# Top-k search of an expert-choice router: bit masks counted by TensorE instead of accumulated comparisons, in one transformer-block kernel

## The chip, the cores and the metric

The kernel runs on one core of a Trainium2 chip. The metric is device time in microseconds, the median of several runs. A core has five engines with their own instruction queues: TensorE (PE in the profile; its weight loads are PEld), VectorE (DVE), ScalarE (ACT), GpSimd (POOL) and SyncE (SP, which here only issues DMAs). They meet through semaphores.

## The reference, cut to what matters

One transformer block over x of shape 8 x 1024 x 256: an attention (16 heads of 64) and then a mixture of experts in which each of 8 experts chooses its K = 512 best tokens out of all 8192:

```
logits = xf @ router_w + router_b           # 8192 x 8
scores = softmax(logits, axis=-1)
G, idx = top_k(scores.T, K)                 # for each expert its 512 best tokens
toks = xf[idx]
h1 = relu(toks @ w1[e] + b1[e])             # 512 x 1024
eo = h1 @ w2[e] + b2[e]                     # 512 x 256
y[idx] += eo * G                            # scattered back
```

Here xf is the normed and modulated attention output; the result is added to x under a gate. The order of the 512 tokens inside an expert does not matter, since their results are added to the rows they came from; ties at the threshold go to the lower token number.

## The kernel before, in words

The work has three parts, in this order.

1. *Attention*, 128 units of work with an order written out by hand. Its last batch also makes the routing scores of the last tokens: `out_route` multiplies with the router (L638), VectorE and ScalarE make the softmax (L643 to L664), and `out_store` has GpSimd copy the scores of 128 tokens into the tile `scores` (L671). Near its start, a small table `steps_of` is made: one row of four candidate offsets for each search step (L784 to L787).
2. *Search and ranks*, the part that is changed. Four transposes (L981) turn `scores` into the PSUM tile `p_sc`: 128 partitions, of which 16 belong to each expert, and 512 scores in each. VectorE copies it to `sc` (L985). The threshold of each expert, the 512th largest score, is then found in 15 steps of two bits, from the top of the fp32 bit pattern (scores are positive, so their order is that of their bits). A step compares all scores with three candidates (L996, each comparison also adds up its hits in a partition into `cnt`), one matmul with the 0/1 matrix `whole_h` adds `cnt` over the 16 partitions of an expert (L1001), `ge` counts how many candidates are reached by at least K scores (L1008), and `cand` is moved up by that many steps (L1013, in the last four steps L1019 and L1020, where float arithmetic would no longer be exact).
   The ranks: masks of scores above and equal to the threshold (L1030), running counts by two scans (L1037, L1043), counts of the partitions before by matmuls with `earlier` and `whole` (L1034, L1035, L1046), and from them the slot of each chosen token; four transposes (L1053) turn the slots back, and `lo` and `hi` are their low five and high bits (L1058, L1059).
3. *Experts*, again in an order written by hand. `entries` (L1075 to L1088) makes one-hot masks of `lo` and `hi`, `choose` (L1099) and `gather` (L1114 to L1123) turn them into token numbers and fetch the rows by indirect DMA; `turn` (L1136), `inner` (L1147) and `outer` (L1159) are the expert's matmuls; the results are added to the output by indirect DMA (L1168). Experts 1 to 7 have their entries made while the expert before them computes; for expert 0 all of it lies between the ranks and its first matmul.

The weights of the first four experts are loaded (L922, L924) while the search runs. In part 2 before the change, the order on each engine is a scheduler's; in the changed kernel, that of the code from the copy of `p_sc` on.

Of the kernel before, what the change touches and what calls it, by code (L numbers as in the profile page):

```python
# [28 lines left out]
F32 = mybir.dt.float32  # L29
BF16 = mybir.dt.bfloat16  # L30
F16 = mybir.dt.float16
I32 = mybir.dt.int32
AF = mybir.ActivationFunctionType
ALU = mybir.AluOpType
AX = mybir.AxisListType
# [3 lines left out]
P = 128  # L39
# [4 lines left out]
def adaln_block(  # L44
# [15 lines left out]
    nc = tc.nc  # L60
    B, S, D = x.shape
    H, _, _, N = w_qkv.shape
    E, _, F = w1.shape
    K = 512
# [6 lines left out]
    KT = K // P  # L71
# [4 lines left out]
    const = ctx.enter_context(tc.tile_pool(name="const", bufs=1))  # L76
    dram = ctx.enter_context(tc.tile_pool(name="dram", bufs=1, space=DRAM))

    ident = const.tile([P, P], F32, name="ident")
# [15 lines left out]

    scores = const.tile([P, KT, E, NTT // KT], F32, name="scores")
    modT = const.tile([P, 2 * KC, B], F32, name="modT")

    steps_of = const.tile([P, 16, 4], I32, name="steps_of")

    mod_d = dram.tile([B, 3 * D], F32, name="mod_d")
    gb_d = dram.tile([B, D], F32, name="gb_d")
# [65 lines left out]
    for i in range(NT // 2):  # L168
        t = work.tile([P, 2, D], F32, tag="p", name=f"x_first{i}", bufs=PB)
# [28 lines left out]
    def mod_silu():  # L198
        pt = ps_m.tile([P, KC, B], F32, tag="mm", name="pt")
        for k in range(KC):  # L200
            nc.tensor.transpose(pt[:, k, :], c_sb[:, k * P : (k + 1) * P], ident[:B, :B])
        nc.scalar.activation(sT, pt, AF.Exp, scale=-1.0)
        nc.vector.tensor_scalar_add(sT, sT, 1.0)
# [87 lines left out]
    def ln_out(b, t):  # L291
# [4 lines left out]
        if b == 0:  # L296
# [5 lines left out]
            for k in range(KC):  # L302
                nc.scalar.activation(  # L303
                    hTs[b][:, k, 2 * t * P : (2 * t + 2) * P], pt[:, k, :], AF.Identity,
                    bias=modT[:, k, b : b + 1], scale=modT[:, KC + k, b : b + 1],
# [463 lines left out]
    with tc.manual_schedule():  # L769
# [10 lines left out]
        ln_norm(0, NT // 2 - 1)  # L780
        for t in parts_of:
            nc.vector.memset(t, 0.0)

        nc.gpsimd.memset(steps_of, 0)  # L784
        nc.gpsimd.iota(steps_of[:, 14, :], pattern=[[1, 4]], base=0, channel_multiplier=0)
        for s in range(14):
            nc.vector.tensor_scalar(  # L787
                steps_of[:, s, :], steps_of[:, 14, :], 28 - 2 * s, None, op0=ALU.logical_shift_left
            )
        g = -1  # L790
        while g < 4 * NSU + LAG or steps:
            u, gm = divmod(g, 4)
# [105 lines left out]
        half = NT // 2  # L898
# [32 lines left out]
    C = NTT // KT  # L931
    lo = rt.tile([P, KT, E, C], I32, name="lo")
    hi = rt.tile([P, KT, E, C], I32, name="hi")
    LO = 32
# [12 lines left out]
    with tc.tile_pool(name="search", bufs=2) as se, tc.tile_pool(  # L947
        name="pos", bufs=1
    ) as po_, tc.tile_pool(name="se_ps", bufs=2, space=PSUM) as sps, tc.tile_pool(
        name="pos_ps", bufs=1, space=PSUM  # L950
    ) as pps:
        for dst, pattern, mult in (
            (iota_lo, [[1, LO]], 0), (iota_hi, [[1, HI]], 0), (part, [[0, 1]], 1),
            (first, [[P, KT], [P * KT, C]], 0),
        ):
            i = po_.tile(list(dst.shape), I32, name=f"i_{dst.name}")
            nc.gpsimd.iota(i, pattern=pattern, base=0, channel_multiplier=mult)
            nc.gpsimd.tensor_copy(dst, i)
        nc.vector.tensor_reduce(
            fold, ident.rearrange("p (g l) -> p l g", l=LO), AX.X, ALU.max  # L960
        )

        whole = po_.tile([P, E, C], F32, name="whole")
        nc.gpsimd.memset(whole, 1.0)
        for base, sign in ((0, 1), (C - 1, -1)):
            nc.gpsimd.affine_select(
                out=whole, in_=whole, pattern=[[-sign * C, E], [0, C]], base=base,
                channel_multiplier=sign, compare_op=ALU.is_ge, fill=0.0,
            )
        whole = whole.rearrange("p e c -> p (e c)")  # L970
        whole_h = po_.tile([P, P], F16, name="whole_h")
        nc.gpsimd.tensor_copy(whole_h, whole)
        earlier = po_.tile([P, P], F32, name="earlier")
        make_upper_triangular(nc, earlier, 1.0, diag=False)
        nc.gpsimd.tensor_mul(earlier, earlier, whole)
        zeros = po_.tile([P, K], F32, name="zeros")
        nc.gpsimd.memset(zeros, 0.0)

        p_sc = pps.tile([P, KT, P], F32, name="p_sc")
        for i in range(KT):  # L980
            nc.tensor.transpose(  # L981
                p_sc[:, i, :], scores[:, i].rearrange("p e c -> p (e c)"), ident
            )
        sc = po_.tile([P, K], F32, name="sc")
        nc.vector.tensor_copy(sc, p_sc.rearrange("p i t -> p (i t)"))  # L985

        cand = se.tile([P, 4], I32, tag="cand", name="cand")
        nc.vector.tensor_copy(cand, steps_of[:, 0, :])  # L990
        for s in range(15):
            bit = 28 - 2 * s
            cnt = se.tile([P, 3], F16, tag="cnt", name=f"cnt{s}")
            for k in range(3):
                above = se.tile([P, K], F32, tag="above", name=f"above{s}_{k}")
                nc.vector.tensor_scalar(  # L996
                    above, sc, cand.bitcast(F32)[:, k + 1 : k + 2], 0.0,
                    op0=ALU.is_ge, op1=ALU.add, accum_out=cnt[:, k : k + 1],
                )
            pc = sps.tile([P, 3], F32, tag="pc", name=f"pc{s}")  # L1000
            nc.tensor.matmul(pc, whole_h, cnt, start=True, stop=True)  # L1001
            base = se.tile([P, 4], I32, tag="base", name=f"base{s}")
            nc.vector.tensor_tensor(
                base, cand[:, :1].to_broadcast([P, 4]), steps_of[:, s + 1, :], ALU.bitwise_or
            )
            ge = se.tile([P, 3], F32, tag="ge", name=f"ge{s}")
            num = se.tile([P, 1], F32, tag="num", name=f"num{s}")
            nc.vector.tensor_scalar(  # L1008
                ge, pc, float(K), 0.0, op0=ALU.is_ge, op1=ALU.add, accum_out=num
            )  # L1010
            cand = se.tile([P, 4], I32, tag="cand", name=f"cand{s}")
            if bit >= 8:
                nc.vector.scalar_tensor_tensor(  # L1013
                    cand, num.to_broadcast([P, 4]), float(1 << bit), base,
                    op0=ALU.mult, op1=ALU.add,
                )
            else:
                inc = se.tile([P, 1], I32, tag="inc", name=f"inc{s}")
                nc.vector.tensor_scalar(inc, num, float(1 << bit), None, op0=ALU.mult)  # L1019
                nc.vector.tensor_tensor(  # L1020
                    cand, base, inc.to_broadcast([P, 4]), ALU.bitwise_or
                )
        thr = cand.bitcast(F32)[:, :1]


        gt = po_.tile([P, K], F32, name="gt")
        eq = po_.tile([P, K], F32, name="eq")
        n2 = po_.tile([P, 2], F32, name="n2")
        for m, i, op in ((eq, 1, ALU.is_equal), (gt, 0, ALU.is_gt)):
            nc.vector.tensor_scalar(  # L1030
                m, sc, thr, 0.0, op0=op, op1=ALU.add, accum_out=n2[:, i : i + 1]
            )
        p_n = pps.tile([P, 2], F32, name="p_n")
        nc.tensor.matmul(p_n[:, 1:2], earlier, n2[:, 1:2], start=True, stop=True)  # L1034
        nc.tensor.matmul(p_n[:, 0:1], whole, n2[:, 0:1], start=True, stop=True)  # L1035
        up = po_.tile([P, K], F32, name="up")
        nc.vector.tensor_tensor_scan(up, zeros, eq, 0.0, ALU.add, ALU.add)  # L1037
        rest = po_.tile([P, 1], F32, name="rest")
        nc.vector.tensor_scalar(rest, p_n[:, 0:1], -1.0, float(K), op0=ALU.mult, op1=ALU.add)
        nc.vector.tensor_sub(rest, rest, p_n[:, 1:2])  # L1040
        nc.vector.scalar_tensor_tensor(eq, up, rest, eq, op0=ALU.is_le, op1=ALU.mult)

        nc.vector.tensor_tensor_scan(up, gt, eq, 0.0, ALU.add, ALU.add)  # L1043
        nc.vector.tensor_add(gt, gt, eq)
        p_up = pps.tile([P, 1], F32, name="p_up")
        nc.tensor.matmul(p_up, earlier, up[:, K - 1 :], start=True, stop=True)  # L1046
        off = po_.tile([P, 1], F32, name="off")
        nc.vector.tensor_copy(off, p_up)
        nc.vector.scalar_tensor_tensor(up, up, off, gt, op0=ALU.add, op1=ALU.mult)

        p_no = pps.tile([P, KT, P], F32, name="p_no")
        for i in range(KT):
            nc.tensor.transpose(p_no[:, i, :], up[:, i * P : (i + 1) * P], ident)  # L1053
        slot = po_.tile([P, KT, E, C], I32, name="slot")
        nc.vector.tensor_scalar_add(
            slot, p_no.rearrange("p i (e c) -> p i e c", e=E), -1.0
        )
        nc.vector.tensor_single_scalar(lo, slot, LO - 1, op=ALU.bitwise_and)  # L1058
        nc.vector.tensor_single_scalar(  # L1059
            hi, slot, LO.bit_length() - 1, op=ALU.arith_shift_right  # L1060
        )

    ew = ctx.enter_context(tc.tile_pool(name="ework", bufs=2))
    ps_ids = ctx.enter_context(tc.tile_pool(name="ps_ids", bufs=1, space=PSUM))
# [166 lines left out]
```

## Time and profile before

| | us |
|---|---|
| time, median of 3 runs (lowest, highest) | 3546.07 (3545.62, 3549.22) |
| the profiled execution's own time | 3549.73 |
| its span, first to last instruction | 3548.0 |
| search, first copy to last threshold (from 3232.32 to 3275.01) | 42.69 |
| ranks, to the transposes of the slots (to 3281.53) | 6.52 |
| from there to the first expert's first matmul (to 3301.0) | 19.5 |
| experts, to the end | 247.0 |

Mean granted TensorE clock: 0.987 of full speed.

How to read the profile: a row of a group gives line, engine, operation, output<-input by the program's names, shapes, count, then busy time, mean nanoseconds of one, and idle time of the engine ahead of it with what ended it. A row of the timeline gives start and duration in us first, and in brackets the idle time before. "128*64" in front of a matmul's shape is the part of the TensorE array that its weights take: 128 rows, 64 columns. A comparison with accumulation shows as two instructions, TENSOR_SCALAR_CACHE_REDUCE and DVE_READ_ACCUMULATOR.

### The profile page before, as it was taken

To read this page: it belongs to the slowest core of one execution; us is meant where nothing else is said; L and a number is where in the kernel's file an instruction comes from. 1 tells how busy PE (TensorE), PEld (TensorE's weight loads), DVE (VectorE), ACT (ScalarE), POOL (GpSimd) and SP (SyncE) were. 2 spreads that over 40 slices of the span, in tenths; PEclk is the share of its full clock that TensorE was granted. 3 is DMA by queue.
4 is the path that set the end of the run, shared out by engine and by line. 5 is a ranking of instruction groups with operands and counts; after the bars stand their busy time and mean duration, and the time that the engine had idled before them with its cause. 6 is when DMAs were issued, how large, how long until landed. Compare 5 with 4: busy or idle time off the path is not lost. (4 is left out here: it accounts for less than half of the span.)

```text
span 3548.0 us, 54197 instructions
## 1 busy us (share of the span) xinstructions
PE 3434.0 (97%) x20631; PEld 1444.1 (41%) x20631; DVE 2863.3 (81%) x3611; ACT 2437.4 (69%) x2996; POOL 2657.8 (75%) x1533
## 2 busy tenths in 40 slices
PE   8999999999999999999999999999999999993898
PEld 3333333334433443334433443344433444432566
DVE  6888888888888888888888888888888888887332
ACT  5877877777777777777777777777777777760111
POOL 3788777978788888977788888977788888881233
PEclk9999999999999999999999999999999999996899
DMA  4011012011220113111211113011211112124342
GB/s 79 13 43 31 25 46 65 26 44 44 63 53 27 51 51 65 31 40 50 59 51 31 48 52 64 31 40 52 58 50 31 52 47 58 49 77 152 94 103 42
DMA packets 190136, 185.39 MB, mean 52 GB/s; under 512 B 49308, under 2 KB 167596, under 8 KB 189748
## 3 DMA queue, kind: packets, MB, share of 16 engines
q1 hardware_dynamic: 173916, 160.54, 16.6%
q0 software_dynamic: 7168, 12.72, 1.8%
q10 hardware_dynamic: 8792, 8.67, 0.8%
q8 instruction: 162, 2.65, 0.3%
q14 instruction: 98, 0.80, 0.1%
HBM read 127.06 MB, written 63.21 MB: 54 GB/s over the span
## 5 line engine op out<-in xcount | busy, mean ns | idle before, releaser
L466 POOL TENSOR_TENSOR acc<-acc,p 128x1024 f32<-128x1024 f32 x764 | 1811.8, 2371 | 350.8 <-ACT p L438 317.7
L382 ACT COPY p<-s 128x1024 f32<-128x1024 f32 x1024 | 994.8, 1019 | 401.6 <-PE s L373 384.1
L435 DVE TENSOR_TENSOR p<-p,less 128x1024 f32<-128x1024 f32 x1024 | 1206.2, 1209 | 28.2 <-PE less L432 25.7
L387 DVE TENSOR_TENSOR top<-top,s 128x1024 f32<-128x1024 f32 x768 | 936.7, 1220 | 269.0 <-ACT p L382 228.0
L438 ACT ACTIVATE p<-p 128x1024 f32<-128x1024 f32 x1024 | 1041.6, 1057 | 73.3 <-DVE p L435 73.0
L373 PE MATMUL s<-qk,qk 64*128 64x512 f32 x4096 | 1020.3, 611 | 15.4 <-DVE parts L413 12.3
L447 PE MATMUL av<-p,v 128*64 128x512 f32 x4096 | 969.1, 593 | 1.8 <-ACT oT L456 1.8
L373 PEld LDWEIGHTS s<-qk,qk 64*128 64x128 f32 x4096 | 359.2, 186 | 512.9 <-issue 223.0
L338 PE MATMUL pq<-hT,wq 128*64 128x512 f32 x2048 | 498.3, 608 | 2.2 <-ACT hT L303 2.2
L447 PEld LDWEIGHTS av<-p,v 128*64 128x64 f32 x4096 | 279.7, 137 | 456.4 <-issue 355.7
L463 POOL TENSOR_TENSOR acc<-p,p 128x1024 f32<-128x1024 f32 x128 | 304.2, 2377 | 163.0 <-ACT p L438 163.0
L338 PEld LDWEIGHTS pq<-hT,wq 128*64 128x64 f32 x2048 | 125.1, 136 | 341.6 <-issue 205.5
L355 PE MATMUL pv<-wq,hT 128*64 128x256 f32 x2048 | 249.2, 385 | 0.0
L1151 ACT ACTIVATE h<-ph,b_sb 128x512 f32<-128x512 f32 (+1 forms) x72 | 46.1, 640 | 255.2 <-PE ph L1147 255.2
L583 PE MATMUL po<-wo,ot 128*64 128x256 f32 x1792 | 205.7, 382 | 0.0
L355 PEld LDWEIGHTS pv<-wq,hT 128*64 128x64 f32 x2048 | 135.7, 136 | 152.3 <-issue 61.2
L405 DVE TENSOR_REDUCE tt<-tt 128x8 f32<-128x1024 f32 x112 | 137.7, 1230 | 56.4 <-PE tt L394 56.2
L387 DVE TENSOR_TENSOR top<-p,s 128x1024 f32<-128x1024 f32 x128 | 155.6, 1215 | 12.2 <-ACT p L382 12.2
L394 PEld LDWEIGHTS tt<-ident,top 128*128 128x128 f32 x1024 | 109.6, 140 | 109.8 <-DVE top L387 109.8
L528 POOL TENSOR_TENSOR oT<-oT,rb 128x1024 f32<-128x1024 f32 x63 | 151.0, 2397 | 0.0
L583 PEld LDWEIGHTS po<-wo,ot 128*64 128x64 f32 x1792 | 123.6, 137 | 66.1 <-issue 9.4
L394 PE MATMUL tt<-ident,top 128*128 128x128 f32 x1024 | 139.9, 280 | 4.7 <-DVE top L387 4.6
(185 smaller groups left out, 2291.5 us busy)
## 6 DMA issues: line engine op xcount, KB each, us to landing
rb<-rden_d SPq DMA_DIRECT2D x126, 256.0 KB
oT_d<-oT SPq DMA_DIRECT2D x62, 512.0 KB
ot<-oT_d SPq DMA_DIRECT2D x56, 512.0 KB
rows_d<-row SPq DMA_DIRECT2D x64, 132.0 KB
rows_d<-gb_d SPq DMA_DIRECT2D x8, 1024.0 KB
w<-in_L_ffn_w_dram ACTq DMA_DIRECT2D x8, 1024.0 KB
w<-in_L_ffn_w_dram SPq DMA_DIRECT2D x8, 1024.0 KB
lnx<-in_L_attn_inputs_dram SPq DMA_DIRECT2D x28, 256.0 KB
```

The source lines that it names most:

```text
L338: nc.tensor.matmul(pq[m * N : (m + 1) * N, :], wq_of(k, a, 2 * p + m), hTs[b][:, k, sl], start=(k == 0), stop=(k == KC - 1),)
L355: nc.tensor.matmul(pv[m * N : (m + 1) * N, i, :], hTs[b][:, k, t0 : t0 + N], wq_of(k, 2, 4 * g, 4), start=(k == 0), stop=(k == KC - 1),)
L373: nc.tensor.matmul(ps[:, j, :], kt[r, c * P : (c + 1) * P], qt[r, h * QB : (h + 1) * QB], start=True, stop=True,)
L382: nc.scalar.copy(probs[u, c], ps)
L387: nc.vector.tensor_tensor(tops[u], probs[u, 0] if c == 1 else tops[u], ps, ALU.max)
L394: nc.tensor.transpose(turned[u][:, 4 * j + t, :], top[:, j, t * P : (t + 1) * P], ident)
L435: nc.vector.tensor_tensor(probs[u, c], probs[u, c], less[u], ALU.add)
L438: nc.scalar.activation(probs[u, c], probs[u, c], AF.Exp)
L447: nc.tensor.matmul(avs[u][j * N : (j + 1) * N, :], v[:, c, hh * N : (hh + 1) * N], pT[:, j, :], start=(c == 0), stop=(c == NT - 1),)
L463: nc.gpsimd.tensor_tensor(sums[u], pts[0], pts[1], ALU.add)
L466: nc.gpsimd.tensor_tensor(sums[u], sums[u], pt, ALU.add)
L583: nc.tensor.matmul(po[m * N : (m + 1) * N, :], ot[:, p, m * N : (m + 1) * N], wo[:, p, :], start=(p == 0), stop=(p == NP - 1),)
```

## The change

The fp32 bit pattern is split into `top`, its bits 14 to 29, and `low`, its lower 14 bits plus one, both as uint16. A first search finds the threshold of `top` in 8 steps; then each score gets a 16-bit `key`: 65535 where its top is above that threshold, `low` where it is equal, 0 elsewhere; a second search of 7 steps finds the threshold of `key`. So there are again 15 steps of two bits with three candidates each. A comparison now writes a bf16 mask and adds nothing up: TensorE does, with 64 columns of a mask as weights and the 0/1 matrix `mine` (partition by expert) as data, so that a step has 24 such matmuls into `pt`; the counts are copied to bf16, and one matmul with `ones_b` adds them over all partitions. Every partition then has the counts of all experts, and `ge` picks its own by `mine_of`. Candidates are fp32 numbers below 65537 throughout. The ranks work on 16-bit masks; the number of scores above the threshold is added up by ScalarE. The table `steps_of`, the copy `sc`, and the matrix `whole_h` go.

The core of the diff:

```diff
-        nc.gpsimd.memset(steps_of, 0)
-        nc.gpsimd.iota(steps_of[:, 14, :], pattern=[[1, 4]], base=0, channel_multiplier=0)
-        for s in range(14):
-            nc.vector.tensor_scalar(
-                steps_of[:, s, :], steps_of[:, 14, :], 28 - 2 * s, None, op0=ALU.logical_shift_left
-            )
...
-        whole_h = po_.tile([P, P], F16, name="whole_h")
-        nc.gpsimd.tensor_copy(whole_h, whole)
...
-        zeros = po_.tile([P, K], F32, name="zeros")
+        zeros = po_.tile([P, K], BF16, name="zeros")
         nc.gpsimd.memset(zeros, 0.0)
+        NS = 3
+        mine = po_.tile([P, E], BF16, name="mine")
+        nc.gpsimd.tensor_copy(mine, whole.rearrange("p (e c) -> p e c", e=E)[:, :, 0])
+        mine_of = po_.tile([P, NS, E], F32, name="mine_of")
+        nc.gpsimd.tensor_copy(mine_of, mine.unsqueeze(1).to_broadcast([P, NS, E]))
+        ones_b = po_.tile([P, P], BF16, name="ones_b")
+        nc.gpsimd.memset(ones_b, 1.0)
+        upto = po_.tile([P, NS + 1], F32, name="upto")
+        upto_i = po_.tile([P, NS + 1], I32, name="upto_i")
+        nc.gpsimd.iota(upto_i, pattern=[[1, NS + 1]], base=0, channel_multiplier=0)
+        nc.gpsimd.tensor_copy(upto, upto_i)
...
-        for s in range(15):
-            bit = 28 - 2 * s
-            cnt = se.tile([P, 3], F16, tag="cnt", name=f"cnt{s}")
-            for k in range(3):
-                above = se.tile([P, K], F32, tag="above", name=f"above{s}_{k}")
-                nc.vector.tensor_scalar(
-                    above, sc, cand.bitcast(F32)[:, k + 1 : k + 2], 0.0,
-                    op0=ALU.is_ge, op1=ALU.add, accum_out=cnt[:, k : k + 1],
-                )
-            pc = sps.tile([P, 3], F32, tag="pc", name=f"pc{s}")
-            nc.tensor.matmul(pc, whole_h, cnt, start=True, stop=True)
...
+            bits = p_sc.rearrange("p i t -> p (i t)").bitcast(I32)
+            LB = 14
...
+            nc.vector.tensor_single_scalar(half[:, 0, :], bits, LB, op=ALU.logical_shift_right)
+            nc.vector.tensor_copy(top, half[:, 0, :])
+            def low_bits():
+                nc.vector.tensor_single_scalar(half[:, 1, :], bits, (1 << LB) - 1, op=ALU.bitwise_and)
+            def low_short():
+                nc.vector.tensor_scalar(low, half[:, 1, :], 1.0, None, op0=ALU.add)
+            def search(key, nb, least, beside):
+                cand = se.tile([P, NS + 1], F32, tag="cand", name=f"cand{least}")
                 nc.vector.tensor_scalar(
+                    cand, upto, float(1 << (nb - 2)), float(least), op0=ALU.mult, op1=ALU.add
                 )
+                for s in range(nb // 2):
...
+                    reach = se.tile([P, NS, K], BF16, tag="reach", name=f"reach{n}")
+                    for k in range(NS):
+                        nc.vector.tensor_scalar(
+                            reach[:, k, :], key, cand[:, k + 1 : k + 2], None, op0=ALU.is_ge
+                        )
+                    pt = sps.tile([P, NS, E], F32, tag="pt", name=f"pt{n}")
+                    for k in range(NS):
+                        for i in range(KT):
+                            for r in range(0, P, N):
+                                nc.tensor.matmul(
+                                    pt[r : r + N, k, :],
+                                    reach[:, k, i * P + r : i * P + r + N], mine,
+                                    start=(i == 0), stop=(i == KT - 1),
+                                )
+                    if s < len(beside):
+                        beside[s]()
+                    base = se.tile([P, NS + 1], F32, tag="base", name=f"base{n}")
+                    nc.vector.tensor_scalar(
+                        base, upto, float(1 << bit) / 4, cand[:, :1], op0=ALU.mult, op1=ALU.add
+                    )
+                    cnt = se.tile([P, NS, E], BF16, tag="cnt", name=f"cnt{n}")
+                    nc.vector.tensor_copy(cnt, pt)
+                    pc = sps.tile([P, NS, E], F32, tag="pc", name=f"pc{n}")
+                    nc.tensor.matmul(pc, ones_b, cnt, start=True, stop=True)
...
+                    nc.vector.scalar_tensor_tensor(
+                        ge, pc, float(K), mine_of, op0=ALU.is_ge, op1=ALU.mult, accum_out=num
+                    )
...
+            t_top = search(top, 30 - LB, 0, (low_bits, low_short))
...
+            nc.vector.tensor_scalar(
+                more, top, t_top, float((1 << 16) - 1), op0=ALU.is_gt, op1=ALU.mult
+            )
+            nc.vector.scalar_tensor_tensor(key, top, t_top, low, op0=ALU.is_equal, op1=ALU.mult)
+            nc.vector.tensor_tensor(key, key, more, ALU.max)
+            thr = search(key, LB, 1, ())
...
+            nc.vector.tensor_scalar(gt, key, thr, None, op0=ALU.is_gt)
+            nc.vector.tensor_scalar(eq, key, thr, None, op0=ALU.is_equal)
...
+            nc.scalar.activation(spare, gt, AF.Copy, accum_out=n_gt)
+            p_n = pps.tile([P, 1], F32, name="p_n")
+            nc.tensor.matmul(p_n, whole, n_gt, start=True, stop=False)
+            up = po_.tile([P, K], F32, name="up")
+            nc.vector.tensor_tensor_scan(up, zeros, eq, 0.0, ALU.add, ALU.add)
+            nc.tensor.matmul(p_n, earlier, up[:, K - 1 :], start=False, stop=True)
+            fits = po_.tile([P, K], BF16, name="fits")
+            nc.vector.tensor_scalar(fits, up, p_n, float(K), op0=ALU.add, op1=ALU.is_le)
+            nc.vector.tensor_tensor(eq, eq, fits, ALU.mult)
...
+            nc.vector.scalar_tensor_tensor(up, up, p_up, gt, op0=ALU.add, op1=ALU.mult)
```

## The prediction

> **What bounds the kernel now.** I read the page first (busy shares, slices), then the waits around the search, the stages, the timeline of one search step, and the rows nearest to the new instructions. The chain that ended last names only the last three pieces and does not help here.
>
> ```profile
> PE 3434.0 (97%) x20631; PEld 1444.1 (41%) x20631; DVE 2863.3 (81%) x3611; ACT 2437.4 (69%) x2996; POOL 2657.8 (75%) x1533
> ...
> PE   8999999999999999999999999999999999993898
> ...
> PEclk9999999999999999999999999999999999996899
> ```
>
> TensorE is busy nearly throughout; the one hole is the slice with the 3. The waits give its reason: GpSimd's first gather waits 60 us for the token numbers, which the search and the ranks make.
>
> ```profile
> POOL erow L1123 <- DVE tok L1119: 60.1, 1, 60.1
> ```
>
> ```profile
> core 0: us, PE busy (x) PEld busy (x) DVE busy (x) ACT busy (x) POOL busy (x), PEclk, DMA share, GB/s
> 3219.00:3232.32 13.32, 6.81 (x62) 4.13 (x59) 8.28 (x36) 2.54 (x8) 7.54 (x30) 0.67 0.46 149
> 3232.32:3275.01 42.69, 2.46 (x15) 1.46 (x14) 38.65 (x155) 0.00 (x0) 0.00 (x0) 0.50 0.57 207
> 3275.01:3281.53 6.52, 1.76 (x7) 1.51 (x7) 6.29 (x12) 0.00 (x0) 0.00 (x0) 0.50 0.00 1
> ```
>
> Each row begins with a stage and its length. Row two is the search (first copy to last threshold), row three the ranks. VectorE is busy, all else idle: one serial chain. What follows (TensorE without a gap from 3301 to 3535 us) waits for its end, so a microsecond here is a microsecond of the kernel. One step, of 15:
>
> ```profile
> 3235.80 0.75 DVE L996 TENSOR_SCALAR_CACHE_REDUCE above<-sc,cand 128x512 f32<-128x512 f32 x1
> ...
> 3236.47 0.74 DVE L996 TENSOR_SCALAR_CACHE_REDUCE above<-sc,cand 128x512 f32<-128x512 f32 x1
> ...
> 3237.14 0.74 DVE L996 TENSOR_SCALAR_CACHE_REDUCE above<-sc,cand 128x512 f32<-128x512 f32 x1
> ...
> 3237.94 0.16 PE L1001 MATMUL pc<-cnt,whole_h 128*128 128x3 f16 x1 [2.58 <-DVE above L996]
> ...
> 3238.14 0.16 DVE L1008 TENSOR_SCALAR_CACHE_REDUCE ge<-pc 128x3 f32<-128x3 f32 x1 [0.18 <-PE pc L1001]
> ...
> 3238.35 0.16 DVE L1013 SCALAR_TENSOR_TENSOR cand<-num,base 128x4 int32<-128x4 f32 x1
> ```
>
> The next step's first comparison starts at 3238.55: 2.75 us a step, of which 2.0 is three comparisons at a pitch of 0.67. The last four steps take 2.94 (one instruction more, L1019). 11 x 2.75 + 4 x 2.94 = 42.0 us.
>
> **The change, part by part.**
>
> *A comparison.* 16-bit in and out, no accumulator. The nearest row is a 16-bit tensor_scalar with a scalar from memory, over 1024 elements:
>
> ```profile
> L1088 DVE TENSOR_SCALAR ids<-at_hi,part 128x1024 bf16<-128x1024 bf16 x8 | 3.8, 480 | 0.0
> L1058 DVE TENSOR_SCALAR lo<-slot 128x512 int32<-128x512 int32 x1 | 0.4, 426 | 0.0
> ```
>
> and how close independent neighbours follow each other, in the timeline:
>
> ```profile
> 3283.41 0.43 DVE L1058 TENSOR_SCALAR lo<-slot 128x512 int32<-128x512 int32 x1
> 3283.75 0.42 DVE L1059 TENSOR_SCALAR hi<-slot 128x512 int32<-128x512 int32 x1
> ```
>
> L1088 can only be four elements a cycle: at two and 0.96 GHz its elements alone would take 533 ns. 480 less the 133 ns of 512 elements gives 347 ns, and independent neighbours overlap by 0.09 (L1059 starts 0.34 after L1058, which lasts 0.43): a pitch of 0.26. The third ends 0.87 us after the first begins. That row is bf16; no row has uint16. The Trainium skill's VectorE: DVE Perf Modes, What auto-detection actually checks, asks only for 16-bit tensors at step 1, so I take the row. Bounds: 0.39 pitch at two a cycle, 0.67 at one.
>
> *Counting on TensorE*, 24 loads of 64 columns with 8-column matmuls, eight after each comparison:
>
> ```profile
> 3165.95 0.41 PE L419 MATMUL pn<-ident_b,parts 128*64 128x128 bf16 x8 [1.19 <-DVE parts L413]
> ...
> 3289.41 0.69 PE L1099 MATMUL pi<-ids,hot 128*32 128x32 bf16 x64 [6.77 <-DVE ids L1088]
> ...
> 3228.28 1.03 PE L638 MATMUL pl<-rw,h2T 128*64 128x8 f32 x16 [0.73 <-ACT h2T L628]
> ```
>
> L419 has the same loads: eight in 0.41, of which one lasts 0.22, a pitch of 27 ns. L1099 (32 columns, granted clock 0.50) shows 8 ns, and 0.66 us at clock 1.00, so the clock hardly counts. L638 is the dear end: 55 ns in f32 at clock 0.50. Against the change speaks the Trainium skill, TensorE: Matmul & The Clock Gate, section Wait — 56ns, not 53.3ns?: starts never closer than about 25 ns, and about 62 ns when the sequencer decodes. 62 would make 24 pairs 1.49 us a step, longer than the comparisons: 0.7 us more a step, 11 in all, and the sum below would be +5 instead of -5.8. L1099's 8 ns lies under both figures, so the row decides: 27. Then eight pairs (0.22) fit inside a comparison and only the last eight show: 0.06 wait + 7 x 0.027 + 0.17 = 0.42.
>
> *A step after:* 0.87 + 0.42 + 0.06 to VectorE + 0.19 copy of the counts (as L1105, 192 ns) + 0.05 + 0.18 matmul with ones_b + 0.04 + 0.23 (ge and its accumulator, 0.21 above, 21 elements more) + 0.20 = 2.24 us. base lies under the counting (0.13 of 0.42). Gain: 11 x 0.51 + 4 x 0.70 = **8.4 us**.
>
> *Before the first step.* GpSimd queues mine, ones_b, mine_of, an iota and a copy ahead of the last scores copies (L671, at 3231.34, no idle before), and drops whole_h (0.26): neighbours there go at 0.11 to 0.20, so +0.5 (0.2 if the bf16 zeros are cheaper). The shift replaces the copy sc (0.69 both from PSUM); then top (0.43 as L1058, 0.69 at worst) and cand: +0.55. **+1.05.** The first two transposes now stand ahead of the pl matmuls on TensorE; their inputs are there at 3227.8, pl's at 3228.25: at most 0.1, not counted.
>
> *Beside the steps.* low_bits (0.69, from PSUM) stands between comparisons and the copy of the counts in step 0, longer than the counting: **+0.17.** low_short (0.43) in step 1 is covered by it (0.17 if slow).
>
> *Between the searches.* more 0.26, key as scalar_tensor_tensor 0.75 (L1041: 750 ns), 0.04, maximum to the start of cand 0.35, cand and wait 0.20: **+1.6** (0.26 more if the maximum runs as L1044, 691 ns).
>
> *Ranks, 6.52 now.* gt and eq 0.61, 0.04, scan 1.22 (L1037; two cycles an element, 16 bits don't help), then the count by earlier now hangs on the scan: 0.69 (from scan end to VectorE, as with p_up). fits 0.48 (0.75), 0.04 + 0.43 (0.69), 0.04 + scan 1.22, 0.69, final 0.75 + 0.06: 6.27. **-0.25** (+0.28 at the dear ends). ScalarE's count of gt (about 0.7 + reading) and the matmul behind it (0.58) end about as the scan does; the ScalarE queue is free then (its last weight load was issued by 3243.6), and its copies and exponentials alternate all through attention without a reload. Cover gone, its excess would show.
>
> *Costs nothing:* the removed steps_of table: 14 instructions in 1.0 us at 14.6 us, after which VectorE idles until 23.0; two GpSimd instructions beside it. SP's queue is unchanged, no DMA is added; the eight DMA waits in front of the first load on TensorE stand there before too. A new step puts 48 more instructions on TensorE behind waits for VectorE, but nothing else is queued there.
>
> **Sum:** -8.4 + 1.05 + 0.17 + 1.6 - 0.25 = **-5.8 us**. Profiled execution: 3549.73 (span 3548.0), to 3543.9. It stands 3.7 above the median of the runs, 3546.07, which becomes **3540.3**. About 0.2%, 7.1 us, is what a measurement of this kernel can tell from no change: the gain is likely below that.
>
> **The rivals.**
> 1. *TensorE becomes the bound of a step.* At a pitch p the counting ends at 0.41 + 23p + 0.17 if it cannot keep up. Break-even is 0.38 us a step more, p = 47 ns; from 68 ns on the kernel is slower by over 0.2%. At L638's 55 ns: +0.55 x 15, net +2.5. For it: 24 loads a step, clock 0.50, and no row of this very form. Against: L419 and L1099.
> 2. *The 16-bit comparison runs slower.* At two a cycle: +0.40 x 15 = +6.0, net +0.2. At one (uint16 unpacked): +1.21 x 15 = +18, net +12.4, 3558. **This is the case on the other side**: one instruction, 45 times, from a pitch of 0.39 there is no gain left, from 0.55 on a loss of over 0.2%. Against: L1088.
> 3. *Cheaper than summed.* Loads at 16 ns (twice L1099): -0.08 x 15 = -1.2; GpSimd's prologue 0.3 less; overheads hidden between small instructions 0.05 a step, 0.75: net -8, 3538. For it: L1099's rate. Warm-up of the experts' first matmuls (3301 to 3305 at clock 0.50, some 2 us) could only be saved if TensorE stayed warm over the ranks, and 8 us of idling in between speak against.
> 4. *It doesn't do what it says:* no sign; the instruction order has 45 comparisons, 360 counting pairs, one mask each.
>
> **How the numbers follow.** Main case 0.63 (its own range 3538 to 3543; 0.14 of it beyond -7.1); rival 1: 0.14 (0.04 slower); rival 2: 0.11 (0.06 slower); rival 3: 0.12, all faster. Faster 0.26, same 0.64, slower 0.10. The range goes from 3536.5 (rival 3 with all dear ends cheap) to 3548.5 (rival 1 near its 55 ns, or two a cycle with slow small pieces); what is left out is mostly the slow comparison.
>
> **What would show it.** Comparison rows near 0.35 us at a pitch of 0.26; steps of 2.2 to 2.3 us; a group of eight counting matmuls in 0.36; search and ranks from the first VectorE read of p_sc to p_no in about 43 us (49.2 now); scores copies at 3231.8. Wrong: comparisons of 0.48 or 0.74; TensorE working on well after the third comparison; a wait of TensorE for anything but VectorE; ranks over 6.8 us.

## The result, and the profile after

The changed kernel takes 3543.49 us, the median of 20 runs (3540.73 to 3545.21), where the kernel before, run beside it, takes 3547.15 (3545.56 to 3550.43): a ratio of 0.9987, with a 95% interval of 0.9981 to 0.9993. The kernel is faster, by 2.5 to 6.7 us. The prediction had 3540.3, with a range from 3536.5 to 3548.5, and had called a gain too small to be told from none the likeliest. The profiled execution takes 3543.85 us, against 3543.9 in the prediction's sum.

The page of the changed kernel, first the busy time of each engine, then TensorE's row of the 40 slices:

```profile
PE 3446.4 (97%) x20991; PEld 1456.2 (41%) x20991; DVE 2847.9 (80%) x3566; ACT 2437.0 (69%) x2998; POOL 2655.7 (75%) x1535
...
PE   8999999999999999999999999999999999995898
```

The slice that showed a 3 for TensorE shows a 5. That isn't the speed of anything that bounds the kernel: TensorE now works through 360 small loads in it. What counts is how long GpSimd's first gather waits for the token numbers, in the waits of GpSimd (in total, times, longest):

```profile
POOL erow L1157 <- DVE tok L1153: 98.9, 8, 53.7
```

The longest wait falls from 60.1 to 53.7 us. The stages of the changed kernel, the search in row one and the ranks in row two:

```profile
core 0: us, PE busy (x) PEld busy (x) DVE busy (x) ACT busy (x) POOL busy (x), PEclk, DMA share, GB/s
3232.91:3269.42 36.51, 16.23 (x375) 13.79 (x375) 26.83 (x130) 0.00 (x0) 0.00 (x0) 0.50 0.65 237
3269.42:3275.67 6.25, 1.76 (x6) 1.50 (x6) 5.16 (x8) 0.72 (x2) 0.00 (x0) 0.50 0.00 0
```

Search and ranks together: 42.76 us, 49.21 before. VectorE is busy for 26.8 of the 36.5 us now, since it waits twice in a step for TensorE's counts. One step in the timeline (start, duration, and in brackets the idle time before and what ended it):

```profile
3238.80 0.88 DVE L1015 TENSOR_SCALAR reach<-top,cand 128x512 bf16<-128x512 uint16 x3
3239.20 0.82 PEld L1023 LDWEIGHTS <-reach 128*64 128x64 bf16 x24 [1.30 <-DVE reach L1015]
3239.21 0.90 PE L1023 MATMUL pt<-mine,reach 128*64 128x8 bf16 x24 [0.87 <-DVE reach L1015]
3239.59 0.22 DVE L1031 TENSOR_SCALAR base<-upto,cand 128x4 f32<-128x4 f32 x1
3240.04 0.10 PEld L1037 LDWEIGHTS <-ones_b 128*128 128x128 bf16 x1
3240.16 0.18 DVE L1035 CAST cnt<-pt 128x24 bf16<-128x24 f32 x1 [0.34 <-PE pt L1023]
3240.39 0.18 PE L1037 MATMUL pc<-cnt,ones_b 128*128 128x24 bf16 x1 [0.28 <-DVE cnt L1035]
3240.61 0.18 DVE L1040 SCALAR_TENSOR_TENSOR ge<-pc,mine_of 128x24 f32<-128x24 f32 x1 [0.27 <-PE pc L1037]
...
3240.83 0.16 DVE L1044 SCALAR_TENSOR_TENSOR cand<-num,base 128x4 f32<-128x4 f32 x1
3241.03 0.62 DVE L1015 TENSOR_SCALAR reach<-top,cand 128x512 bf16<-128x512 uint16 x2
```

From 3238.80 to 3241.03 is 2.23 us. The three comparisons end 0.88 us after the first begins; counting begins 0.41 in, and TensorE is done soon after the third. Of the 1.35 us that follow the comparisons, VectorE waits 0.34 and 0.27: this chain of small pieces is now more than half of a step.

### The profile page after: what moved, and what is told of

It is laid out like the page before. It is cut to its first block, busy times and chain, and to the rows that moved or that the text cites. A ratio compares the mean times of both kernels' runs of the same rounds, so it can differ in the third digit from the quotient of the medians.

```text
span 3542.1 us, 54875 instructions
## 1 busy us (share of the span) xinstructions
PE 3446.4 (97%) x20991; PEld 1456.2 (41%) x20991; DVE 2847.9 (80%) x3566; ACT 2437.0 (69%) x2998; POOL 2655.7 (75%) x1535
```

## The experiments

The kernel's time alone carries a scatter of some 1.5 us (standard deviation of one kernel's runs, 1.2 to 1.9), which no edit causes; it comes from ahead of the search and from the experts behind it, as told below. So each profile is read by two lengths that this scatter does not touch: *start*, from VectorE's first product that writes the last router scores (into `row` or, in one experiment, into `scores`) to its first read of `p_sc`, and *stretch*, from that read to `p_no`. "Sum" is the two together, less the same two of the kernel before, in us.

| kernel | start | stretch | sum | ratio to before (95%) |
|---|---|---|---|---|
| before | 1.62 | 49.21 | | |
| changed | 2.28 | 42.77 | -5.8 | 0.9987 (0.9981 to 0.9993) |
| 16-bit keys, accumulating | 2.10 | 50.80 | +2.1 | 1.0007 (0.9999 to 1.0016) |
| fp32 keys, masks counted | 1.63 | 47.57 | -1.6 | 0.9998 (0.9989 to 1.0006) |
| counting doubled | 2.27 | 50.72 | +2.2 | 1.0009 (1.0001 to 1.0018) |
| loads of 128 columns | 2.28 | 41.18 | -7.4 | 0.9978 (0.9969 to 0.9987) |
| scores by VectorE | 1.21 | 42.76 | -6.9 | 0.9982 (0.9976 to 0.9989) |
| both of these | 1.20 | 41.20 | -8.4 | 0.9978 (0.9970 to 0.9987) |
| three bits a step | 2.33 | 43.07 | -5.4 | 0.9986 (0.9979 to 0.9992) |
| changed, again | 2.28 | 42.76 | -5.8 | 0.9985 (0.9979 to 0.9992) |
| 128 columns, again | 2.29 | 41.15 | -7.4 | 0.9981 (0.9973 to 0.9988) |
| both, again | 1.21 | 41.15 | -8.5 | 0.9977 (0.9968 to 0.9985) |

### One part alone: 16 bits, but accumulating comparisons

```diff
+                    cnt = se.tile([P, NS], F16, tag="cnt", name=f"cnt{n}")
                     nc.vector.tensor_scalar(
-                        reach[:, k, :], key, cand[:, k + 1 : k + 2], None, op0=ALU.is_ge
+                        reach[:, k, :], key, cand[:, k + 1 : k + 2], 0.0,
+                        op0=ALU.is_ge, op1=ALU.add, accum_out=cnt[:, k : k + 1],
                     )
...
-                    pc = sps.tile([P, NS, E], F32, tag="pc", name=f"pc{n}")
-                    nc.tensor.matmul(pc, ones_b, cnt, start=True, stop=True)
+                    pc = sps.tile([P, NS], F32, tag="pc", name=f"pc{n}")
+                    nc.tensor.matmul(pc, whole_h, cnt, start=True, stop=True)
```

> One part alone: the 16-bit keys and the split into two searches stay, but each comparison adds up its hits again (accumulator) and one matmul with whole_h adds the partitions, as before. Theory A (what makes the comparison fast is that it no longer accumulates; 16 bits alone do nothing for it): comparison rows near 0.74 us at a pitch of 0.67, steps of 2.75 us, from VectorE's first read of p_sc to the transposes of the slots 42.8 + 15 x 0.51 + 0.4 (low_bits and low_short less covered) = about 51 us, kernel some 8 us above the changed one, 2 above the one before. Theory B (16-bit operands are what counts): rows near 0.35, steps of 1.55 us, the stretch some 33 us, kernel 10 us below the changed one.

The groups by form of this kernel (count, then busy us and mean ns of one):

```profile
L1012 DVE TENSOR_SCALAR_CACHE_REDUCE reach<-top,cand 128x512 bf16<-128x512 uint16 x24 | 16.6, 743 | 0.3
```

743 ns, as the fp32 comparison of the kernel before: the accumulating form does not get faster with 16-bit operands. A step stays at 2.74 to 2.75 us, and since splitting the pattern costs its price, the stretch grows to 50.80 us. The 16 bits alone are a loss.

### The other part alone: fp32 scores, masks counted by TensorE

```diff
-                    above, sc, cand.bitcast(F32)[:, k + 1 : k + 2], 0.0,
-                    op0=ALU.is_ge, op1=ALU.add, accum_out=cnt[:, k : k + 1],
+                        reach[:, k, :], sc, cand.bitcast(F32)[:, k + 1 : k + 2], None, op0=ALU.is_ge
...
+                            nc.tensor.matmul(
+                                pt[r : r + N, k, :],
+                                reach[:, k, i * P + r : i * P + r + N], mine,
+                                start=(i == 0), stop=(i == KT - 1),
+                            )
```

> The other part alone: the fp32 scores and the single 30-bit search stay, but the comparisons write bf16 masks without accumulating and TensorE counts them (24 loads of 64 columns, mine, ones_b, mine_of as in the changed kernel). Theory A (a comparison without accumulator runs at two fp32 elements a cycle): rows near 0.48 us, pitch 0.39, steps of 2.63 us (2.82 in the last four), stretch from the first read of p_sc to the transposes of the slots 49.2 - 1.8 = 47.4 us, kernel 1 to 2 us below before. Theory B (fp32 masks run at one a cycle): rows of 0.74, steps of 3.4 us, stretch about 59 us, kernel 10 us above before.

```profile
L1001 DVE TENSOR_SCALAR reach<-sc,cand 128x512 bf16<-128x512 f32 x45 | 19.2, 483 | 0.5
```

The same comparison without the accumulator, still on fp32 input: 483 ns, and in the changed kernel 350. The step is 2.63 us (2.82 in the last four), the stretch 47.57 (expected 47.4). The search of this kernel also runs in the order of its code, as in the changed one. So of the 6.4 us by which the stretch shrinks in the whole change, leaving the accumulator brings 1.6; what remains exists only with both, as 16 bits pay off only in the form that doesn't accumulate. The sums of the two parts alone, -1.6 and +2.1, do not add up to the -5.8 of both.

### The suspected cost doubled: every mask counted twice

```diff
-                        for i in range(KT):
-                            for r in range(0, P, N):
-                                nc.tensor.matmul(
...
+                        for _ in range(2):
+                            for i in range(KT):
+                                for r in range(0, P, N):
+                                    nc.tensor.matmul(
```

Each mask's counting group is issued a second time and overwrites the first.

> The changed kernel with the counting matmuls of every comparison issued twice (the second set overwrites the first with the same sums): 48 loads a step instead of 24. Theory A (pairs go at 27 ns and 24 of them keep up with the comparisons, 48 do not): the counting ends at 0.41 + 47 x 0.027 + 0.20 = 1.88 us after a step's start instead of 1.30; steps of 2.8 us, kernel about 8.5 us above the changed one. Theory B (the pairs are issue-bound near 16 ns or less and 48 still keep up): steps of 2.35 us, kernel 2 us above. Theory C (a fixed cost per matmul of 60 ns, hidden only partly now): steps of over 4 us, kernel 27 us above or more.

A step of it in the timeline:

```profile
3249.03 1.44 PE L1024 MATMUL pt<-mine,reach 128*64 128x8 bf16 x48 [0.87 <-DVE reach L1015]
...
3250.52 0.18 DVE L1036 CAST cnt<-pt 128x24 bf16<-128x24 f32 x1 [0.88 <-PE pt L1024]
```

TensorE runs without a break here. One matmul lasts about 0.195, so (1.44 - 0.195) / 47 = 26.5 ns a matmul in the mean, where the prediction took 27 from L419. They do not start one by one at that distance. Two views of the end of this row, the second opened after two more matmuls have ended:

```profile
3250.23 0.25 PE L1024 MATMUL pt<-mine,reach 128*64 128x8 bf16 x4
3250.28 0.19 PE L1024 MATMUL pt<-mine,reach 128*64 128x8 bf16 x2
```

The last two matmuls, one for each half of the 128 columns, fill the same 0.19 us, and the two before them start 0.05 us earlier. In the whole search two halves start within 7 ns of each other, mostly at once, and the next two follow 53 to 55 ns behind (73 to 76 behind the first two of a step). L419 is built the same way, so 27 was the right price.

With 48 loads VectorE waits 0.88 us instead of 0.34, and the step is 2.77 us. This is rival 1 made real: at twice the loads TensorE is the bound and the sum turns from a gain into a loss. In the changed kernel it is not: eight loads (0.21 us) fit under one comparison's pitch of 0.265.

### One size changed: twelve loads of 128 columns a step

```diff
-                            for r in range(0, P, N):
-                                nc.tensor.matmul(
-                                    pt[r : r + N, k, :],
-                                    reach[:, k, i * P + r : i * P + r + N], mine,
-                                    start=(i == 0), stop=(i == KT - 1),
-                                )
+                            nc.tensor.matmul(
+                                pt[:, k, :], reach[:, k, i * P : (i + 1) * P], mine,
+                                start=(i == 0), stop=(i == KT - 1),
+                            )
```

> The changed kernel with 128 columns of a mask as weights, 12 matmuls a step instead of 24 of 64 columns. Theory A (a load costs by its columns, and loads run beside matmuls): pitch about 54 ns, the last four of a step end as now, steps of 2.2 to 2.25 us, no difference of the kernel beyond 0.5 us. Theory B (loads of all 128 columns cannot run beside the matmul before them, as those of the two column halves can): pitch over 0.1 us, last group 0.1 to 0.2 us later, kernel 2 to 3 us above the changed one. Theory C (bf16 loads of 128 columns are faster per column): steps 0.05 to 0.1 us shorter, kernel about 1 us below.

The load's group in this kernel, and then in the changed one:

```profile
L1022 PEld LDWEIGHTS <-reach 128*128 128x128 bf16 x180 | 8.3, 107 | 25.7 <-DVE reach L1015 23.3
```

```profile
L1023 PEld LDWEIGHTS <-reach 128*64 128x64 bf16 x360 | 12.2, 149 | 22.0 <-DVE reach L1015 22.0
```

Twice the columns load in less time. The last matmuls of a step's row, seen like those above, are single:

```profile
3248.18 0.19 PE L1022 MATMUL pt<-mine,reach 128*128 128x8 bf16 x2
3248.21 0.17 PE L1022 MATMUL pt<-mine,reach 128*128 128x8 bf16 x1
```

One of 128 columns starts every 26 to 29 ns behind the first of its group, where two of 64 columns took 53 together: half the time for the same mask. The Trainium skill, TensorE: Matmul & The Clock Gate, section Weight-path perf modes — Fast Weight Load (FWL) and DoubleRow, says that weights of 128 that are not fp32 are loaded in a faster way without being asked; these rows agree. It shows in the step's timeline:

```profile
3247.58 0.79 PE L1022 MATMUL pt<-mine,reach 128*128 128x8 bf16 x12 [0.87 <-DVE reach L1015]
...
3248.41 0.18 DVE L1033 CAST cnt<-pt 128x24 bf16<-128x24 f32 x1 [0.22 <-PE pt L1022]
```

VectorE waits 0.22 instead of 0.34 us for the counts; the step is 2.12. This is Theory C, at the upper end of its 0.05 to 0.1 us a step; Theory A's pitch of 54 ns is twice the measured one. Fifteen of them make the 1.6 us by which the stretch is shorter. The prediction's rival 3 hoped for loads at 16 ns a pair; cheaper loads exist, but in another shape than the change uses.

### The changed kernel's later start: last scores written by VectorE

```diff
+        if b * NT + t == NTT - 2:
+            for i in range(2):
+                ct, ci = divmod(NTT - 2 + i, KT)
+                nc.vector.tensor_scalar_mul(scores[:, ci, :, ct], ex[:, i, :], den[:, i : i + 1])
...
-            nc.gpsimd.tensor_copy(scores[:, ci, :, ct], row[:, D:])
+            if tt != NTT - 2:
+                nc.gpsimd.tensor_copy(scores[:, ci, :, ct], row[:, D:])
```

> The change, with the last two score columns written by VectorE straight into scores (two 8-element products ahead of the ones that go into row), in place of the two copies on GpSimd that stand behind its longer list of constants. In the changed kernel the first VectorE read of p_sc starts 2.28 us after the first product into row starts (3230.63 to 3232.91), in the kernel before 1.62 us. Theory A (the GpSimd list is what made the search start later): the transposes wait only for the two products, 0.64 us, and the read comes about 1.4 us after the first product starts, so 0.9 us sooner than in the changed kernel; the stretch from that read to p_no stays 42.8, and the time goes 0.9 us below the changed kernel's. Theory B (the later start came from elsewhere, such as the transposes that now stand ahead of the pl matmuls on TensorE): the read still comes about 2.2 us after the first product.

The end of GpSimd's list in the changed kernel, then VectorE's timeline in this experiment:

```profile
3231.61 0.12 POOL L978 IOTA upto_i<- 128x4 int32 x1
3231.80 0.19 POOL L979 CAST upto<-upto_i 128x4 f32<-128x4 int32 x1
3231.93 0.33 POOL L670 COPY scores<-row 128x8 f32<-128x8 f32 x2
```

```profile
3229.73 0.64 DVE L664 TENSOR_SCALAR scores<-ex,rd 128x8 f32<-128x8 f32 x2
3230.28 0.38 DVE L667 TENSOR_SCALAR row<-ex,rd 128x8 f32<-128x8 f32 x2
3230.94 0.69 DVE L1000 TENSOR_SCALAR half<-p_sc 128x512 int32<-128x512 int32 x1 [0.28 <-PE p_sc L988]
```

GpSimd goes from constants straight to the copies of the scores, 0.7 us after VectorE has finished them (3230.63 + 0.64). With these copies gone, the read of `p_sc` comes 1.21 us after the first product instead of 2.28, and waits 0.28. So the later start was GpSimd's queue (Theory A). The transposes ahead of `pl` cost nothing that shows: in the kernel with fp32 keys two of them stand there too (3228.14, `pl` 3228.76), and its start is 1.63, as before the change. The stretch is unchanged.

### Both edits that shorten it

> The change with both edits that shorten it: scores written by VectorE, and twelve loads of 128 columns a step instead of 24 of 64. If the two savings lie on the chain one behind the other: first read of p_sc 1.4 us after the first product, stretch to p_no 41.2, together 2.5 us below the changed kernel and about 7.5 us below the kernel before, ratio 0.9979. If the earlier start only makes a wait elsewhere longer, the stretch grows by what the start gains, and the time is that of the 128-column version alone, ratio 0.9982.

Start 1.20, stretch 41.20: the savings add up in the trace, with no longer wait behind. The kernel's time is another matter, since the median of 3540.8 lies no lower than the 3540.02 of the 128 columns alone, measured at another time. So both were run once more, on one chip:

> The version with twelve loads of 128 columns once more, beside the next kernel on the same chip. The stretch from the first read of p_sc to p_no is 41.2 within 0.1 and the read comes 2.28 us after the first product, as before. If the stretch is what counts, the time is 1.6 below the changed kernel and some 6 us below the kernel before: ratio 0.9982 within 0.0005.

> Both edits once more, beside the 128-column version alone. Theory A (the earlier start of the search is worth its 1.07 us of the trace in the kernel's time): median 1.07 below the run beside it, within the 1.0 that medians of some 20 runs scatter. Theory B (what is saved ahead of the search is lost again, since later work waits for something else): no difference, or the other way, and the wait would be seen between p_no and the first matmul of the experts, which is 19.4 us in the changed kernel.

3540.92 (17 runs) and 3540.27 (12 runs), ratios 0.9981 and 0.9977 to the kernel before. The lengths repeat to 0.05 us, and the medians have the expected sign; 0.65 or 1.07 us cannot be told apart by them. Theory B's wait is not there: from `p_no` to the first matmul of the experts it is 19.4 us with both edits too. With both edits the medians lie 7 to 8 us below those of the kernel before (the intervals of the ratios reach from 4.6 to 11.4), and the ratios lie below both of the changed kernel, though the intervals overlap.

### Another size changed: three bits a step

```diff
-        NS = 3
+        NS = 7
...
-            LB = 14
+            LB = 15
...
-                for s in range(nb // 2):
+                for s in range(nb // 3):
...
-                    bit = nb - 2 - 2 * s
+                    bit = nb - 3 - 3 * s
...
-                        base, upto, float(1 << bit) / 4, cand[:, :1], op0=ALU.mult, op1=ALU.add
+                        base, upto, float(1 << bit) / 8, cand[:, :1], op0=ALU.mult, op1=ALU.add
```

> The change with three bits a step: seven masks instead of three, ten steps instead of 15, the searches split 15 and 15 bits. It tests the split of a step into comparisons and the rest. Theory A (a comparison costs its pitch of 0.265, the counting only shows behind the last one, and the rest of a step is fixed): a step is 2.23 + 4 x 0.265 + 0.05 for the longer copies = 3.34 us, ten of them 33.4 against 33.5, and the stretch from the first read to p_no 42.8 within 0.5. Theory B (the counting adds up, 56 loads at 27 ns, and shows): 0.5 us or more above that in each step, stretch 48 or more. Theory C (the comparisons overlap more in a longer row of them, or the fixed part is larger than 1.35): stretch 41 or less.

```profile
3246.16 1.93 DVE L1015 TENSOR_SCALAR reach<-top,cand 128x512 bf16<-128x512 uint16 x7
3246.57 1.95 PE L1023 MATMUL pt<-mine,reach 128*64 128x8 bf16 x56 [0.91 <-DVE reach L1015]
...
3248.57 0.22 DVE L1035 CAST cnt<-pt 128x56 bf16<-128x56 f32 x1 [0.34 <-PE pt L1023]
```

Seven comparisons take 1.93 us, 0.265 each behind the first, and the wait for the counts is 0.34 as with three. A step is 3.38 us (expected 3.34), the stretch 43.07 (expected 42.8). Two bits or three, the same: the four more comparisons and longer copies cost 1.15 us in each of ten steps, and that uses up what the five steps saved bring, 2.23 each. The split of a step that the prediction made thus holds at a second size.

### The changed kernel again, and where the scatter comes from

> The changed kernel once more, unaltered, to see what of its time no edit moves. Theory A (the search is settled, what comes ahead of it is not): the stretch from the first read of p_sc to p_no is 42.8 within 0.1 again, the experts behind it 247 us within 0.3, but the first read of p_sc comes at any time from 3230.5 to 3233.5, as the last batch's row of reciprocals lands sooner or later at 3196 to 3199, and with it goes the kernel's time. Theory B (the later start of the search belongs to the change): the first read comes at 3232.9 within 0.3, and the ratio to the kernel before is the same 0.9987 within 0.0002.

Start and stretch repeat to 0.01 us, but the first read of `p_sc` comes at 3234.33, 1.42 us later than in the first profile of the same kernel, and beyond the span that was expected; the profiled execution takes 3545.37, 1.52 longer, with nothing changed in the code. Two profiles show best what goes with it: the last batch's normalisation (`oT`, VectorE, L557), which by the code waits for a row of reciprocals (`rb_last`) that comes back through DMA, and TensorE's busy time and granted clock around it. (The rows put the end of the wait down in part to `rows_d`, a later transfer of the same queue.) First the changed kernel again, its VectorE timeline and its stages:

```profile
3199.19 1.29 DVE L557 TENSOR_TENSOR oT<-oT,rb_last 128x512 f32<-128x512 f32 x2 [6.19 <-DMA rows_d<-row]
```

```profile
3190.00:3200.00 10.00, 6.15 (x60) 3.82 (x58) 1.22 (x4) 0.00 (x0) 0.00 (x0) 0.94 0.46 124
3200.00:3210.00 10.00, 10.00 (x68) 6.03 (x70) 6.83 (x18) 0.00 (x0) 4.56 (x10) 0.72 0.37 123
```

and then the kernel with both edits (its first profile):

```profile
3196.59 0.69 DVE L557 TENSOR_TENSOR oT<-oT,rb_last 128x512 f32<-128x512 f32 x1 [4.18 <-DMA rows_d<-row]
3198.30 0.69 DVE L557 TENSOR_TENSOR oT<-oT,rb_last 128x512 f32<-128x512 f32 x1 [1.03 <-DMA rb_last<-rden_last]
```

```profile
3190.00:3200.00 10.00, 8.82 (x84) 5.62 (x82) 1.79 (x4) 0.00 (x0) 0.00 (x0) 1.00 0.53 154
3200.00:3210.00 10.00, 8.91 (x92) 5.67 (x90) 7.31 (x19) 0.58 (x1) 5.79 (x12) 1.00 0.26 86
```

In the one, the products start at 3199.19, TensorE has idled for nearly 4 of the 10 us before 3200, and in the next 10 it runs at a granted clock of 0.72 without a gap. In the other the first product starts at 3196.59, TensorE idles 1.2 us, and the clock stays at 1.00. All twelve profiles fall in line: where the first product starts by 3197.3 (four of them), the clock of the second stretch is 1.00 and the last scores are made at 3228.5 to 3229.0; where it starts from 3197.9 on (eight), the clock is 0.72 to 0.87 and the scores come at 3229.7 to 3232.1. What lets the row of reciprocals land sooner or later was not tried; the kernel with both edits shows both, 1.00 in its first profile and 0.87 in its second, so no edit decides it.

A second part of the scatter lies behind `p_no`. From the experts' first matmul to the end the twelve profiles take 245.9 to 247.1 us, and the length falls as the granted clock of the first 6 us after that matmul rises, from 0.62 to 0.82. The two ends, the changed kernel again and the 128-column version again:

```profile
3296.60:3302.60 6.00, 6.00 (x10) 2.67 (x10) 5.65 (x5) 0.71 (x2) 0.00 (x0) 0.62 0.02 4
3291.54:3297.54 6.00, 6.00 (x13) 2.81 (x13) 5.65 (x5) 1.38 (x2) 0.00 (x0) 0.82 0.00 1
```

TensorE is busy throughout in both. In each profile the clock goes from 0.50 to 1.00 within these 6 us, here sooner and there later; two profiles of the kernel with both edits differ by 0.55 us in the length of the experts. What sets the moment stays open.

## Why the prediction was right

By its own steps, between the two profiled executions:

- **Steps, -8.4.** The first search's eight steps take 18.03 us (3234.17 to 3252.20) with `low_bits` in them, the second's seven 15.63 (3253.79 to 3269.42); less 0.16 for `low_bits` that is 33.5, 2.23 a step. Before, from the first comparison to the last threshold, it was 41.96. Measured -8.5. The comparison is 350 ns (347 worked out) at a pitch of 0.265 (0.26), so the bf16 row L1088 was the right price for uint16, and rival 2 is out. The cycle behind that price comes out of the rows: 512 more elements cost an fp32 TENSOR_TENSOR 529 ns (L1044 691, L387 1220), so 1.03 ns for one element, and from 350 ns for 512 elements here to the 480 of L1088 for 1024 it is 0.25 ns, a quarter. Beside the 16-bit tensors at step 1 that the prediction names, the same section (the Trainium skill, VectorE: DVE Perf Modes, What auto-detection actually checks) asks for a single source and a destination in SBUF, with outermost sizes that are even or equal, if four are to go in a cycle. The keys and masks, in SBUF and of 512 elements, meet that, and the 350 ns agree.
- **Before the first step, +1.05.** The start is 0.66 longer (+0.5 predicted, from GpSimd's queue, which the fifth experiment confirms: the copies of the scores begin 1.30 us after the first product, before the change 0.64), and from the first read to the first comparison it takes 1.26 where it was 0.73 (+0.53; 0.55 predicted). Measured +1.2: the bf16 `zeros` brought nothing.
- **low_bits, +0.17.** Step 0 takes 2.39 us, step 1 2.24: +0.16 and, for `low_short`, nothing.
- **Between the searches, +1.6.** From the start of `more`, 3252.20, to the next comparison, 3253.79: 1.59. The maximum took the cheaper of its two prices (0.42).
- **Ranks, -0.25.** 6.25 us against 6.52: -0.27. The wait for the count by `earlier` (0.68 after the scan) is there as worked out, and ScalarE's count of `gt` stays under the scan.

Together -5.8, as predicted. The rest of the difference of 5.9 lies outside the change: the last scores come 0.07 sooner, and the experts end 0.06 sooner after `p_no`. That the profiled execution met the sum to 0.05 us is luck in so far as these two parts came out alike in the two profiles: over all twelve they scatter by 3.5 and 1.4 us. The lengths inside the search are not luck; they repeat to 0.05 us.

**The rule that spoke against it.** The prediction set L419's 27 ns against the Trainium skill, TensorE: Matmul & The Clock Gate, Wait — 56ns, not 53.3ns?, with about 62 ns where the sequencer decodes and a floor of about 25. The doubled counting has 26.5 ns in the mean, but that is no sign of the floor: two matmuls on the two column halves start within 7 ns of each other, and the next two 53 ns later. As with L1099's 8 ns, a least distance of 25 ns does not hold between matmuls on different columns, and the 62 ns is not seen here. Single matmuls of 128 columns do start 26 to 29 ns apart in the fourth experiment; whether that is the floor or their loads, the runs do not tell. The clock, which "hardly counts" by L1099, does count in fp32: 16 loads and matmuls of L638 take 0.64 us at a granted clock of 1.00 and 1.03 at 0.50. For bf16 loads the reading held.

**What was off.** The median, by 3.2 us, though the sum was right. The step that failed is the last one: "It stands 3.7 above the median of the runs, 3546.07, which becomes **3540.3**". It carries the distance between one profiled execution and the median of three runs over to the changed kernel. The three runs were low: beside the changed kernel the median is 3547.15 (20 runs), and later 3547.67 (38), 3548.17 (64) and 3547.84 (28). So the profiled execution stood 2.6 above the median beside it, which makes 1.1 of the 3.2 us. The other 2.1 come from the distance not being the same for both kernels: the changed kernel's profiled execution stands only 0.4 above its own median, and in its second profile 2.3.

With that step goes the class of the gain: the bound of 0.2%, 7.1 us, was coarse, for 20 runs of each kernel tell 4 us from nothing. The two comparisons in time, 3.7 and 5.1 us between medians, are both below the traces' 5.8, but their intervals hold it (2.5 to 6.7 and 2.8 to 7.5 us). Over all eleven comparisons the ratios follow the sums of the table; taken times 3548 us, they lie about 0.6 us above the sums in the mean (an estimate). The sums all rest on one profile of the kernel before, and whether these tenths are a real loss isn't settled.

## What to carry to other kernels

When a serial stage on VectorE compares and counts, ask first which form the instruction takes: here the accumulator held a comparison at 743 ns in fp32 and in uint16, and only a plain mask with 16-bit operands, counted by an idle TensorE, went to 350. Price such a counting chain by its last group only, as long as one group fits under one comparison, as it did here (0.21 us under 0.265), and give it weights of 128 columns. Where the start of the stage scatters from run to run by more than the gain, measure the stage by lengths between its own instructions, and take the baseline from many runs rather than three.

## What the hardware showed that was not expected

- An accumulating comparison takes 743 ns for 512 elements in 16 bits as in fp32; without the accumulator fp32 to bf16 takes 483 and uint16 to bf16 350.
- A bf16 weight load of 128 columns lasts 107 ns, one of 64 columns 149; with 8-column matmuls, one of 128 starts every 27 ns and two of 64 start together every 53. The load of `ones_b` (0.10 us, 128 columns) stands in every step of the changed kernel's timeline and shows this without an experiment.
- At a granted clock of 0.50, 64 bf16 loads of 32 columns with their matmuls (L1099, kernel before) take 0.69 us and at 1.00 still 0.66, while 16 fp32 loads of 64 columns (L638) take 1.03 us at 0.50 and 0.64 at 1.00.
- A few microseconds' difference in when one row comes back through DMA goes with a granted clock of 1.00 or of 0.72 to 0.87 in the 10 us behind it, and with 3.5 us in when the search can begin.
- The experts' part takes 245.9 to 247.1 us, with a mean clock of 0.82 to 0.62 in its first 6 us.
